# Where GpSimd stops between gathers in a two-layer graph kernel

## The chip, the cores and the metric

The kernel runs on one core of a Trainium2 chip. The metric is the device time of one execution in microseconds (us); lower is better. The kernel before took 847.21 us, the median of three runs (846.74 to 851.41).

## The reference

There are 8 batches of 2048 nodes with 128 features (`x`), and one 2048 x 2048 matrix `adj` that is sparse: the diagonal, and about 8 further entries in a row, placed symmetrically, each with a value of its own.

```python
# layer 0
sj, si = x @ w_j, x @ w_i
res = si[:, :, None] + sj[:, None, :] + adj[None] * w_r + g_b
x = layernorm(x + einsum('bij,bjd->bid', res, x) @ weight + bias)
# layer 1: A = adj, hops of a Chebyshev recursion, A1 = A2 = adj
xs = [x, x A, 2 (x A) A - x, x A, 2 (x A) A - x]
x = layernorm(x + relu(concat(xs) @ Theta1 + bias))
```

In layer 0 the matrix multiplies `x @ weight` (the terms from `si` and `sj` are of low rank and are added as a few rows). Layer 1 becomes two passes over the matrix, here called hops 1 and 2.

## The kernel before, in words

Nodes are cut into 16 chunks of 128; a chunk of all batches is a tile of 128 x 1024 numbers (512 KB). Everything is in 32-bit floats.

The first 150 us load `adj` and `x`, transpose the matrix, find which blocks hold entries, and form Y = `x @ weight` (tiles `Y0` to `Y15`), while chunk 0 of layer 0 is summed along the way. Then a loop `for c in range(ND)` does chunks 1, 2 and 3 of layer 0 with dense products: in step c, TensorE multiplies 16 pairs of tiles for chunk c + 1 (L839, inner loop over j). Beside these products VectorE builds the lists of rows that the other chunks need (`list_round`, L556).

The remaining 12 chunks of layer 0, and all 16 in each hop, use only the rows that matter. For a chunk, seven lists of 128 row numbers are gathered from DRAM: four for strips of 32 nodes, two for strips of 64, one for the whole chunk (`fetch_lists`, L714, which calls `gather`, L640). One gather is one indirect DMA issued by GpSimd; it brings 128 rows of 4 KB into one of nine tiles, `Y0` to `Y8`, used in turn. In layer 0 the rows come from `y0_d` (the profile prints it as `y_d`), in hop 1 from `u_d`, in hop 2 from `y_d`. TensorE multiplies them by the matching rows of the matrix (`listed_rows`, L880).

These matrix rows are gathered too, into four `stage` tiles: `gathers(count, mm)` (L687) takes the next `count` jobs off a list, seven jobs to a chunk, four for the narrow lists and three for the wide ones. In layer 0 they come from `rr_d`; for the four dense chunks, which are needed only from the hops on, from `adj`. With `mm` given, each gather also waits for that matrix product. `keep_r` (L663) multiplies what has landed by a mask on VectorE and moves it to where TensorE reads it. GpSimd runs all gathers in the order in which the program calls them (`behind`, L196, keeps each after the one before).

The order of chunks is `seq`: 9 to 14, then 4 to 8, then 15. In the loop over `seq` each step does: the chunk's own block (L864), `put` (its matrix rows), the wide-list jobs of the next chunk, the listed rows, `make_u` of the chunk before (transposes L184, products L399 and the store of U by ScalarE's queue), then `finish0` (L378: two `tensor_add`, L382, and the layernorm, L204 to L229). Chunk 15 comes last; after it 14 of the 28 jobs of the dense chunks are issued, and the rest in hop 1, two in a step.

A hop opens three chunks (`begin`: L932 and the own block), does the listed rows of the first two, and so on. Within an engine the compiler's scheduler orders instructions by the dependences it is given, except where `keep_in_program_order` or `behind` fix it; so a new dependence can move work on other engines. VectorE and ScalarE read TensorE's results from PSUM, and wait for TensorE's signals to do so.

Of the kernel before, what the change touches and what calls it, by code (L numbers as in the profile page):

```python
# [18 lines left out]
def kernel(  # L19
# [29 lines left out]
    nc = tc.nc  # L49
# [4 lines left out]
    HB = B // 2  # L54
# [7 lines left out]
    ND = 4  # L62
    NG4 = 9

    seq = list(range(NG4, NC - 1)) + list(range(ND, NG4)) + [NC - 1]
    LAST = NC - 1
# [102 lines left out]
    nc.vector.memset(si, 1.0)  # L169

    flip = [0]

    def evict(dst, src, dve=None):
        flip[0] ^= 1
        if flip[0] if dve is None else dve:
            nc.vector.tensor_copy(dst, src)  # L176
        else:
            nc.scalar.copy(dst, src)  # L178

    def transpose4(srcs, name, t=None, dve=None):  # L180

        pt = p_tr.tile([P, 4, P], F32, name=f"pt_{name}", tag="pt")
        for i, s in enumerate(srcs):
            nc.tensor.transpose(pt[:, i, :], s, ident)  # L184
        if t is None:
            t = trp.tile([P, 4, P], F32, name=f"tr_{name}", tag="tr")
        evict(t, pt, dve)
        return t

    def batches_t(src, name, dve=None):  # L190
# [187 lines left out]
    def finish0(c, accs, xr, norm=True):  # L378

        for h in range(2):  # L380
            hs = slice(h * HB, (h + 1) * HB)
            nc.vector.tensor_add(xr[:, hs, :], accs[h], xr[:, hs, :])  # L382
        if norm:
            layernorm(xr, f"0_{c}")
        return xr

    def make_u(c, z, xt, u=None):

        for h in range(2):
            transpose4([z[:, h * HB + i, :] for i in range(4)], f"p{c}_{h}",  # L390
                       xt[:, h * HB:(h + 1) * HB, :])
        if c < ND:
            nc.scalar.dma_start(out=xt_d[c], in_=flat(xt))
        if u is None:
            u = rows4(f"u{c}")
        for h in range(2):
            pp = p_sm.tile([P, HB, D], F32, name=f"pp{c}_{h}", tag="sm")
            for i in range(HB):
                nc.tensor.matmul(  # L399
                    pp[:, i, :], xt[:, h * HB + i, :], th[:, 0, :], start=True, stop=True  # L400
                )
            nc.scalar.copy(u[:, h * HB:(h + 1) * HB, :], pp)
        nc.scalar.dma_start(out=u_d[c * P:(c + 1) * P, :], in_=flat(u))

    def copy_r(n0, n1):
# [275 lines left out]
        (c, q, n) for cs in (seq, range(ND)) for q in (True, False) for c in cs  # L681
        for n in range(4 if q else 3)
    ]
    dense_jobs = 7 * ND
    waiting = []

    def gathers(count, mm=None):  # L687

        for _ in range(count):
            if not jobs:  # L690
                break
            c, q, n = jobs.pop(0)
            if n == 0:
                if len(waiting) == 3:
                    keep_r(*waiting.pop(0))
                waiting.append((
                    c, q, int(c >= ND) + 1,
                    stages[:, turn[1] % 4 * BD:turn[1] % 4 * BD + BD + 4 * TW],
                ))
                turn[1] += 1  # L700
            gather_r(*waiting[-1], n)
            if mm is not None:
                tc.add_manual_dep(
                    order[-1].ins, mm.ins.name,
                    mybir.DependencyInfo(
                        mybir.DependencyClass.Sync, mybir.DependencyReason.DATA
                    ), reason="pace",
                )


    G = [flat(y) for y in Y[:NG4]]
    got = {}

    def fetch_lists(i, src, c, count):  # L714

        gs = got.setdefault((i, c), [])
        ids = [4 * c + t for t in range(4)] + [LP + 2 * c, LP + 2 * c + 1, LF + c]
        if i and c in first:
            src = src[0:LAST * P]
        for n in ids[len(gs):count]:  # L720
            gs.append(G[turn[2] % NG4])
            turn[2] += 1
            gather(gs[-1], src, idx, n, src.shape[0])
        return gs

    def put(c):
# [52 lines left out]
    with nc.allow_non_contiguous_dma(reason="512-byte rows of blocks"):  # L779
        pending, accs, xr = None, acc0, load_x(0, "xr", nc.sync)  # L780
        at1, ar2 = first_at[1], None
        for c in range(ND):
            if c + 1 < ND:
                if NA <= c + 2 < ND:
                    ar2 = load_rows(c + 2, wide[3])
                xr1 = load_x(c + 1, "xr", nc.sync)
            if c < 2:
                copy_r(2 + 5 * c, 7 + 5 * c)
            if 1 <= c <= 2:
                for n in range(8 * c - 8, 8 * c):  # L790
                    tc.keep_in_program_order(
                        nc.sync.dma_start(out=y0_d[n * P:(n + 1) * P, :], in_=flat(Y[n]))
                    )
            if c == 0:
                make_ub()
                more_rows()
                rank1(0, accs, si_t(0))
            else:
                z = finish0(c, accs, xr, c > 2)
            if c + 1 < ND:  # L800
                accs1, sit = acc_pair(), si_t(c + 1)
                at2 = first_at.get(c + 2)
                for j in range(NC):
                    if c == 0:
                        if j == 4:
                            tile_ranks()
                        if j == 7:
                            tile_lists()
                        if j == 10:
                            at = tile_lists_end()  # L810
                            half_ranks()
                        if j == 14:
                            chunk_ranks()
                            z = finish0(c, accs, xr, False)
                            layernorm(z, "0_0", at)
                    if c == 1 and j < 2:
                        candidates(2 * j)
                        candidates(2 * j + 1)
                    if c == 1 and (j > 1 and j % 2 == 0 or j == NC - 1):
                        list_round(j // 2 - (j < NC - 1))  # L820
                    if c == 2:
                        if j == 6:
                            at = chunk_lists_end()
                            layernorm(z1, "0_1", at)
                        if j == 9:
                            layernorm(z, "0_2", at)
                        if j == 8:
                            fetch_own(0, y0_d, seq[0])
                            late0 = fetch_block(0, seq[0])
                    if (c > 0 or j > 11) and not (c == 2 and j > 11):  # L830
                        gathers(1 if j % 4 == 3 else 2, mm)
                    if c == 2 and j > 11:
                        fetch_lists(0, y0_d, seq[0], 2 * j - 22)
                    if ar2 is not None and j % 2 == 0 and j >= 8:
                        if j == 8:
                            at2 = by_chunk(wide[0])
                        transpose_group(c + 2, ar2, at2, j // 2 - 4)
                    for h in range(2):
                        mm = nc.tensor.matmul(  # L839
                            accs1[h], at1[:, j, :], Y[j][:, h * HB:(h + 1) * HB, :],  # L840
                            start=(j == 0), stop=False, skip_group_check=True,
                        )
                rank1(c + 1, accs1, sit)
                if c == 1:
                    gathers(2, mm)
                if c == 2:
                    fetch_lists(0, y0_d, seq[1], NG4 - 7)
                at1, ar2, accs = at2, None, accs1
            if pending is not None:
                make_u(*pending)  # L850
            z1 = z
            pending, xr = (c, z, rows4(f"xt{c}")), xr1
# [37 lines left out]
    with nc.allow_non_contiguous_dma(reason="512-byte rows of a diagonal block"):  # L890
        xr = load_x(seq[0], "xs", nc.sync)
        for c, c1 in zip(seq, seq[1:] + [None]):
# [4 lines left out]
            if c1 is not None:  # L897
                fetch_own(0, y0_d, c1)
                if c1 in first:
                    late0 = fetch_block(0, c1)  # L900
                xr1 = load_x(c1, "xs", nc.sync)
                put(c)
                while any(job[0] == c1 for job in jobs):
                    gathers(1)
            else:
                put(c)
            if c == LAST:
                listed_rows(0, y0_d, c, accs, lambda: make_u(*pending))
            else:
                listed_rows(0, y0_d, c, accs)  # L910
                make_u(*pending)
            z = finish0(c, accs, xr)
            if c == LAST:
                gathers(dense_jobs // 2)
            pending, xr = (c, z, x1t[c], held.get((1, c))), xr1
        for c in hops[:2]:
            fetch_own(1, u_d, c)
# [4 lines left out]
        def hop(i, src):  # L922
# [16 lines left out]
            def end(c, accs):  # L939
# [17 lines left out]
                else:  # L957
# [2 lines left out]
                        out=out[:, c * P:(c + 1) * P, :].rearrange("b p f -> p b f"), in_=z  # L960
                    )

            early = [begin(n) for n in range(3)]
            late = [fetch_block(i, c) for c in first]
            for n in range(2):
# [105 lines left out]
```

## Time and profile before

| | |
|---|---|
| median of three runs | 847.21 us |
| the profiled execution's own time | 891.02 us |
| its span, first to last instruction | 889.2 us |
| mean clock granted to TensorE | 0.965 of full speed |
| TensorE, matrix products | 785.2 us busy, 3631 |
| GpSimd (POOL) | 420.2 us busy, 431 |
| VectorE (DVE) | 360.1 us busy, 1056 |
| ScalarE (ACT) | 176.6 us busy, 429 |
| one gather on GpSimd | 0.99 us, the next starts 1.30 us after it |
| DMA over the span | 264 MB, 297 GB/s |

All durations of engines come from the one profiled execution, which took longer than the runs. In it the dense chunks end at about 273 us, layer 0 at about 493 us, and hop 2 begins at about 709 us. A line of a timeline gives start, busy time, engine, source line, operation, what it writes and reads, how often, and in brackets how long the engine was idle before it and what released it. "remote" or "another core or an unknown queue" stands where no instruction or transfer known to the profile ended at the right moment. A busy interval of GpSimd for a gather is the time in which it issues the gather, not that of the data.

### The profile page before, as it was taken

Reading aid. Unit: us, or ns where it says so; the run is one execution under the profiler, and the core shown is the slowest. Engines: PE = TensorE matmul, PEld = TensorE weight load, DVE = VectorE, ACT = ScalarE, POOL = GpSimd, SP = SyncE. Lnnn points to the kernel's source line nnn. Section 1 sums busy time; section 2 is a strip of 40 time slices with the busy share of each in tenths; the row PEclk is TensorE's granted clock in tenths of the full one; section 3 lists DMA queues with packets and bytes.
Section 4 is the critical chain, followed back from the end, with each engine's and each line's share of the span. In section 5 each row is a group of like instructions: output and inputs, shape, how many; then the busy total and the mean of one; then the engine's idle time right before and its main releaser. Section 6 shows DMA issues by size and latency. Waiting matters only on the chain.

```text
span 889.2 us, 10783 instructions
## 1 busy us (share of the span) xinstructions
PE 785.2 (88%) x3631; PEld 390.2 (44%) x3631; DVE 360.1 (41%) x1056; ACT 176.6 (20%) x429; POOL 420.2 (47%) x431
## 2 busy tenths in 40 slices
PE   5999999999993888799894889998999999999994
PEld 4666654465541533333332533333433434445441
DVE  5555674246960443444441201000100035556666
ACT  3665652001110222221221100000000001111112
POOL 0000000036777267566655475666665456666661
PEclk9999999899997898999997999999999999999998
DMA  8699999892485699899894789999999789999995
GB/s 284 197 312 312 298 299 295 259 364 92 133 305 179 240 340 318 309 334 371 294 355 163 248 266 373 315 329 312 370 382 386 273 308 357 362 342 344 343 351 173
DMA packets 172283, 264.28 MB, mean 297 GB/s; under 512 B 17458, under 2 KB 123226, under 8 KB 170044
## 3 DMA queue, kind: packets, MB, share of 16 engines
q0 software_dynamic: 49280, 147.41, 46.3%
q1 hardware_dynamic: 99610, 88.37, 31.2%
q10 hardware_dynamic: 23330, 27.73, 8.6%
q8 instruction: 31, 0.51, 0.2%
q14 instruction: 32, 0.26, 0.1%
HBM read 242.03 MB, written 60.96 MB: 341 GB/s over the span
## 4 chain that ended last, share of the span: by engine, by line
PE 65%; DMA 11%; issue 8%; DVE 6%; another core or an unknown queue 5%; ACT 3%; POOL 1%; SPq 0%; POOLq 0%; DVEq 0%; ACTq 0%
PE acc L880 26%; PE acc L864 8%; DMA Y<-u_d,idx 6%; PE acc L932 5%; PE acc L839 5%; PE pp L399 4%; PE acc L340 4%; PE acc L330 3%; DMA Y<-y_d,idx 3%; DVE rc L556 2%; PE pt_p L184 2%; PE pt_a L184 2%; DMA rc<-in_adj_dram 1%; PE pt_r L950 1%
## 5 line engine op out<-in xcount | busy, mean ns | idle before, releaser
L641 POOL DMA_INDIRECT Y<-y_d,idx x196 | 194.1, 991 | 141.7 <-PE acc L880 88.1
L880 PE MATMUL acc<-Y,rc 128*32 128x512 f32 (+2 forms) x896 | 227.8, 607 | 17.6 <-DMA Y<-u_d,idx 7.1
L641 POOL DMA_INDIRECT stage<-rr_d,idx x84 | 85.7, 1020 | 222.3 <-PE acc L839 194.2
L641 POOL DMA_INDIRECT Y<-u_d,idx x112 | 111.0, 991 | 76.5 <-PE acc L880 44.4
L880 PEld LDWEIGHTS acc<-Y,rc 128*32 128x32 f32 (+2 forms) x896 | 60.6, 128 | 174.5 <-issue 114.1
L880 PE MATMUL acc<-Y,rct 128*32 128x512 f32 (+2 forms) x336 | 97.6, 619 | 4.0 <-DVE rct L669 3.9
L839 PE MATMUL acc<-Y,wide 128*128 128x512 f32 x192 | 87.9, 608 | 0.0
L864 PE MATMUL acc<-Y,rd 128*128 128x512 f32 x140 | 67.0, 597 | 0.0
L839 PEld LDWEIGHTS acc<-Y,wide 128*128 128x128 f32 x192 | 36.2, 195 | 40.0 <-issue 40.0
L217 ACT ACTIVATE st<-st,epst 128x8 f32<-128x8 f32 x32 | 9.9, 310 | 220.8 <-DVE st L216 100.1
L176 DVE COPY z<-acc 128x512 f32<-128x512 f32 x9 | 6.2, 692 | 117.1 <-remote 33.1
L382 DVE TENSOR_TENSOR xs<-acc,xs 128x512 f32<-128x512 f32 x24 | 16.4, 682 | 75.1 <-PE pp L399 40.4
L880 PEld LDWEIGHTS acc<-Y,rct 128*32 128x32 f32 (+2 forms) x336 | 23.2, 131 | 46.3 <-issue 36.4
L184 PE MATMUL pt_a<-ident,rc 128*128 128x128 f32 x240 | 35.9, 286 | 6.5 <-DMA rc<-in_adj_dram 6.0
L330 PE MATMUL acc<-wx,tr_x 128*128 128x130 f32 x256 | 36.6, 286 | 3.9 <-ACT tr_x L178 3.1
L952 DVE SCALAR_TENSOR_TENSOR z<-z,pt_r 128x512 f32<-128x512 f32 x32 | 20.5, 682 | 47.6 <-PE acc L880 24.4
L301 DVE TENSOR_REDUCE rc<-rc 128x64 f32<-128x2048 f32 x16 | 36.5, 2280 | 7.0 <-DMA rc<-in_adj_dram 7.0
L330 PEld LDWEIGHTS acc<-wx,tr_x 128*128 128x128 f32 x256 | 32.9, 195 | 14.0 <-ACT tr_x L178 6.4
L340 PE MATMUL acc<-Y,wide 128*128 128x512 f32 x64 | 36.1, 646 | 2.5 <-ACT Y L334 1.4
L184 PEld LDWEIGHTS pt_a<-ident,rc 128*128 128x128 f32 x240 | 29.5, 148 | 15.8 <-issue 14.5
L932 PEld LDWEIGHTS acc<-th,wide 128*128 128x128 f32 x256 | 31.7, 194 | 9.8 <-issue 8.8
L309 DVE TENSOR_REDUCE stage<-rct 128x64 f32<-128x2048 f32 x12 | 27.4, 2285 | 20.3 <-ACT rct L178 20.3
(210 smaller groups left out, 918.4 us busy)
## 6 DMA issues: line engine op xcount, KB each, us to landing
rc<-in_adj_dram SPq DMA_DIRECT2D x16, 1024.0 KB
rr_d<-rct SPq DMA_DIRECT2D x12, 1024.0 KB
rr_d<-in_adj_dram SPq DMA_DIRECT2D x12, 1024.0 KB
xs<-in_x_dram SPq DMA_DIRECT2D x20, 512.0 KB
y_d<-Y SPq DMA_DIRECT2D x16, 512.0 KB
out_dram<-z ACTq DMA_DIRECT2D x16, 512.0 KB
u_d<-u ACTq DMA_DIRECT2D x14, 512.0 KB
Y<-y_d SPq DMA_DIRECT2D x14, 512.0 KB
```

The costliest lines, as they stand in the source:

```text
L184: nc.tensor.transpose(pt[:, i, :], s, ident)
L301: nc.vector.tensor_reduce(mk[:, c, :], a.rearrange("p (w f) -> p w f", f=TW), AX.X, ALU.max, apply_absolute_value=True,)
L309: nc.vector.tensor_reduce(mkt[:, :, 4 * c:4 * c + 4], at.rearrange("p j (t f) -> p j t f", f=TW), AX.X, ALU.max, apply_absolute_value=True,)
L330: nc.tensor.matmul(py[:, i, 0:D + 2], xt[b // HB][:, (b + i) % HB, :], wx, start=True, stop=True,)
L340: nc.tensor.matmul(acc0[h], first_at[0][:, c, :], Y[c][:, h * HB:(h + 1) * HB, :], start=(c == 0), stop=False, skip_group_check=True,)
L399: nc.tensor.matmul(pp[:, i, :], xt[:, h * HB + i, :], th[:, 0, :], start=True, stop=True)
L641: g = nc.gpsimd.indirect_dma_start(out=out, out_offset=None, in_=src, in_offset=bass.IndirectOffsetOnAxis(ap=ids[:, n:n + 1], axis=0), bou ...
L839: mm = nc.tensor.matmul(accs1[h], at1[:, j, :], Y[j][:, h * HB:(h + 1) * HB, :], start=(j == 0), stop=False, skip_group_check=True,)
L864: in_order(nc.tensor.matmul(accs[h], r, t[:, h * HB:(h + 1) * HB, :], start=start, stop=stop, skip_group_check=True,))
L880: in_order(nc.tensor.matmul(accs[h][w * t:w * t + w], r[:, o + w * t:o + w * t + w], gs[t][:, h * HB * D:(h + 1) * HB * D], start=False, s ...
L932: in_order(nc.tensor.matmul(accs[h][:, b, :], x1t[c][:, h * HB + b, :], th[:, i, :], start=(b == 0), stop=False, skip_group_check=True,))
L952: nc.vector.scalar_tensor_tensor(z[:, hs, :], z[:, hs, :], 0.0, pt, op0=ALU.max, op1=ALU.add)
```

## The change

It does five things.

1. `evict`, `finish0` and `make_u` now keep the instruction that they issue in a table `done`: the last eviction of a `transpose4`, the second `tensor_add` of a chunk, the last copy of U.
2. A helper `pace` makes the gather that was just issued wait for a given instruction. `gathers` uses it as before for `mm`; `fetch_lists` can use it for its first gather.
3. In the dense loop's step c = 2, matrix-row gathers stop after j = 8, and the first Y0 gathers begin at j = 10 instead of j = 12. Four matrix-row gathers less stand before them: 54 instead of 58.
4. In the loop over `seq`, the first of the next chunk's wide-list gathers waits for the `tensor_add` of the chunk two before the current one (for seq[1] that is chunk 3; seq[0] has none).
5. At the end of layer 0 there were 14 gathers of dense chunks' rows in one go, then nine gathers of U. Now five gathers are issued before chunk 15 is finished, one that waits for its `tensor_add`, and one more; then, as hop 1 opens, four lists of U for the first chunk, three that wait for the last transposed tile's eviction, two lists of the second chunk that wait for the last copy of U, and then seven more gathers of dense chunks' rows.

The data, the arithmetic and the number of gathers are the same. On VectorE, the six `keep_r` instructions that stood before chunk 3's two `tensor_add` now stand after that chunk's layernorm.

```diff
+    done = {}
     def evict(dst, src, dve=None):
         flip[0] ^= 1
         if flip[0] if dve is None else dve:
-            nc.vector.tensor_copy(dst, src)
-        else:
-            nc.scalar.copy(dst, src)
+            return nc.vector.tensor_copy(dst, src)
+        return nc.scalar.copy(dst, src)
...
-        evict(t, pt, dve)
+        done["t"] = evict(t, pt, dve)
...
-            nc.vector.tensor_add(xr[:, hs, :], accs[h], xr[:, hs, :])
+            done[c] = nc.vector.tensor_add(xr[:, hs, :], accs[h], xr[:, hs, :])
...
-            nc.scalar.copy(u[:, h * HB:(h + 1) * HB, :], pp)
+            done["u"] = nc.scalar.copy(u[:, h * HB:(h + 1) * HB, :], pp)
...
-    dense_jobs = 7 * ND
     waiting = []
+
+    def pace(ins):
+
+        tc.add_manual_dep(
+            order[-1].ins, ins.ins.name,
+            mybir.DependencyInfo(mybir.DependencyClass.Sync, mybir.DependencyReason.DATA),
+            reason="pace",
+        )
...
             gather_r(*waiting[-1], n)
             if mm is not None:
-                tc.add_manual_dep(
-                    order[-1].ins, mm.ins.name,
-                    mybir.DependencyInfo(
-                        mybir.DependencyClass.Sync, mybir.DependencyReason.DATA
-                    ), reason="pace",
-                )
+                pace(mm)
...
-    def fetch_lists(i, src, c, count):
+    def fetch_lists(i, src, c, count, step=None):
...
             gather(gs[-1], src, idx, n, src.shape[0])
+            if step is not None:
+                pace(step)
+                step = None
         return gs
...
-                    if (c > 0 or j > 11) and not (c == 2 and j > 11):
+                    if c == 2 and j > 5:
+                        if j < 9:
+                            gathers(2, mm)
+                        elif j > 9:
+                            fetch_lists(0, y0_d, seq[0], 2 * j - 18)
+                    elif c > 0 or j > 11:
                         gathers(1 if j % 4 == 3 else 2, mm)
-                    if c == 2 and j > 11:
-                        fetch_lists(0, y0_d, seq[0], 2 * j - 22)
...
                 put(c)
+                step = done[([ND - 1] + seq)[seq.index(c) - 1]] if c != seq[0] else None
                 while any(job[0] == c1 for job in jobs):
-                    gathers(1)
+                    gathers(1, step)
+                    step = None
...
+            if c == LAST:
+                gathers(5)
             z = finish0(c, accs, xr)
             if c == LAST:
-                gathers(dense_jobs // 2)
+                gathers(1, done[c])
+                gathers(1)
...
+            if i == 1:
+                fetch_lists(i, src, first[0], 4)
+                fetch_lists(i, src, first[0], 7, done["t"])
+                fetch_lists(i, src, first[1], NG4 - 7, done["u"])
+                gathers(7)
             early = [begin(n) for n in range(3)]
```

## The prediction

> **What bounds the kernel now.** I read the page, then the chain of work that ended last, then the timelines of single engines around the chain's two longest pieces. The page first:
>
> ```profile
> PE 785.2 (88%) x3631; PEld 390.2 (44%) x3631; DVE 360.1 (41%) x1056; ACT 176.6 (20%) x429; POOL 420.2 (47%) x431
> ...
> PE 65%; DMA 11%; issue 8%; DVE 6%; another core or an unknown queue 5%; ACT 3%; POOL 1%; SPq 0%; POOLq 0%; DVEq 0%; ACTq 0%
> ```
>
> TensorE carries two thirds of the chain; what the change can reach is in the rest. An "unknown queue" holding 4.7% on a one-core kernel (about 42 us) is odd. The chain in order of time (start, length, what) says where it is:
>
> ```profile
> 269.39 21.39 another core or an unknown queue
> ...
> 470.74 13.03 another core or an unknown queue
> ...
> 513.75 5.30 DMA Y<-u_d,idx
> ```
>
> Two gaps hold 34 us: one where layer 0 leaves its dense chunks (c = 3), one at the last sparse chunk but one. The third line is a price: a 512 KB gather, from its start on GpSimd to its landing. Now the timelines at the first gap (start, busy, engine, line, what, idle before and its releaser):
>
> ```profile
> 272.74 1.09 PE L184 MATMUL pt_p<-ident,xr 128*128 128x128 f32 x8
> ...
> 286.79 0.99 POOL L641 DMA_INDIRECT Y<-y_d,idx  x1 [0.30 <-issue]
> ...
> 290.76 0.69 DVE L382 TENSOR_TENSOR xr<-acc,xr 128x512 f32<-128x512 f32 x1 [21.37 <-remote]
> ...
> 291.08 0.59 ACT L178 COPY xt<-pt_p 128x512 f32<-128x512 f32 x1 [24.59 <-remote]
> ...
> 293.02 3.79 PE L399 MATMUL pp<-th,xt 128*128 128x128 f32 x16 [18.33 <-DVE xt L176]
> ```
>
> TensorE finished the transposes that ScalarE wants at 273.8, and before them the sums that VectorE wants; both readers start 17 us later, within 0.32 us of each other, and TensorE then waits 18.3 us for them. In between GpSimd gathers without a break, its last one ending at 287.78. The second gap has the same shape:
>
> ```profile
> 471.84 0.44 PE L184 MATMUL pt_p<-ident,xs 128*128 128x128 f32 x2
> ...
> 480.82 0.99 POOL L641 DMA_INDIRECT stage<-in_adj_dram,idr  x1 [0.30 <-issue]
> ...
> 483.79 0.69 DVE L176 COPY Y<-pt_p 128x512 f32<-128x512 f32 x1 [13.05 <-remote]
> ...
> 484.54 3.79 PE L399 MATMUL pp<-th,Y 128*128 128x128 f32 x16 [11.26 <-DVE Y L176]
> ```
>
> Readers of TensorE's results resume 3.0 and 2.0 us after GpSimd's last gather. Smaller cases agree: gathers end at 315.80, 330.59, 808.94, 851.29 and a reader on ScalarE or VectorE starts at 317.38, 332.26, 810.34, 852.66 (1.4 to 1.7 us later), though its input had been done for 4 to 8 us. Early in a run of gathers results arrive at once (384.37, two gathers in). So in this execution a long unbroken run of gathers goes with late arrival of TensorE's signals, and a break lets them through. I take that as the trace's rule, not as a known mechanism.
>
> **What the Trainium skill says.** "SBUF — State Buffer", section "SBUF: two separate sides": only VectorE's shared port pair is contended with GpSimd; ScalarE and TensorE have ports of their own. ScalarE waited here as long as VectorE, so the trace doesn't fit a port lock. "Perfetto Trace Analysis", section "Summary: the profiler window per engine type": a TensorE end is an estimate, and a software-issued DMA ends in the record when its descriptors are written, not when data lands. Hence 990 ns for a 512 KB gather, and I take landings from the chain. "DMA: Bandwidth & Descriptors", section "Anatomy of one DMA": 2.0 us plus bytes at 436 GB/s, which would be an estimated 3.2 us for 512 KB; the trace has 5.30, with other transfers beside it, and I use that.
>
> **Part 1, first Y0 gathers sooner.** Of the row gathers of `rr_d`, 58 stood before the first Y0 gather, now 54: the first nine Y0 gathers move up four places. GpSimd starts one every 1.30 us (0.99 busy, 0.30 issue) without waiting there, so Y0 starts at 271.21 instead of 276.42 and the ninth ends at 282.6 instead of 287.8: 5.2 us. The stores they depend on don't hold them: they waited for nothing at 276.42, and the traffic of those stores had faded by 262. Next stands the first gather of chunk 11, which now waits for the second `tensor_add` of chunk 3, so GpSimd stops at 282.6. By the rule VectorE and ScalarE resume 2 to 3 us later, near 285.1 instead of 290.76: 5.7 us sooner. VectorE's `keep_r` work moves behind chunk 3's layernorm; its six products are 1.2 us and TensorE needs them only in the 64-row products about 10 us on: nothing. At the resumed end three `stage` gathers stand before the five Y0 gathers of chunk 10 (none before), but those wait for TensorE reading their buffers, 11 us later: hidden. One gather more (three for chunk 12, two before) then delays chunk 11 by 1.3 us. Left: 4.4 to 5.7, I take **4.8 us**.
>
> **Part 2, one pause per chunk.** The first row gather of chunk seq[k+1] waits for the add of seq[k-2]. Behind it on GpSimd stand two row gathers and the lists of the chunk. In the even stretch from 372 to 457 the row gather starts at 387.95 and the add ends at 389.80: 1.85 us of pause each. GpSimd idles 2.51 us per chunk there, waiting for TensorE to free buffers; that shrinks to about 0.7. The period is 15.19 us, TensorE's products and a 1.35 us wait for the layernorm, so the pause costs nothing; without that idle time it would cost up to 1.85 x 8 = 15 us. Before 345 the add is already done when GpSimd arrives: no pause and no gain.
>
> **Part 3, end of layer 0.** Of 14 `stage` gathers after the last lists (463.92 to 481.81) five stay; the sixth waits for chunk 15's add. GpSimd stops at 470.1, so the copy at 483.79 starts at about 472.3, when its input is done: 11.5 us. The end of chunk 15's products goes from 492.2 to 480.7 and its add from 492.9 to 481.5. Then two gathers (to 484.1), four of U (to 489.3), three behind `done["t"]`, two behind `done["u"]`. Those steps shift from 501.8 and 506.7 to 487-491 and 491-495. The last two end near 498, and seven `stage` gathers (7 x 1.30 = 9.1 us) follow, to 507. Only then come the five U gathers of chunk 10, which started at 512.46. TensorE could have freed their buffers by 501; the seven in front of them eat 6 of the 11.5. Left: **5.5 us**.
>
> Sum: 4.8 + 0 + 5.5 = 10.3 us of the profiled execution's 891.0 (span 889.2 and 1.8 around it), so 880.7. That execution is 43.8 us, 5.2%, over the median of the runs, 847.2. Is the stall in the plain runs too? The trace can't say. It is the value that decides. Bounds: all of it there (10.3 gained) or none (below). I take all of it, since nothing in the trace ties the stall to recording: 847.2 - 10.3 = **836.9**.
>
> **Rivals.** *The stalls belong to the profiled execution (0.35, ends slower).* For it: the unknown queue's 42 us nearly equals the 43.8 us between profile and median. Against it: TensorE emits as many records in the even stretch, where the readers are seldom late. Without stalls, GpSimd's order alone counts. Part 1 gives 1.3 us (17 gathers instead of 18 up to chunk 10's lists), at most 4.5. In part 3 chunk 15's products end at about 479, U's first nine gathers are all out by 493.5 before the change and 496 after it; before, the next five start when buffers come free at 496.5, after it behind the seven `stage` gathers at 505: 8.5 us lost, in a stretch (530 to 575) where TensorE is 90% busy and gives nothing back. Net 4 to 7: about 852 us, 846 to 855. If a share f of the stalls is real, the sum is 10.3f - 5.5(1 - f): slower begins below f = 0.35.
>
> *A wait takes the place of the one removed (0.15).* GpSimd resumes right behind the add, and the next run of gathers makes signals late again (from 304 to 345 runs of nine or ten do so, and no pause falls there). Or U's seven `stage` gathers cost the whole of part 3. One of the two gains is left: 842, 839 to 848.
>
> *The pauses don't pause.* In the even stretch the wait is 1.85 us at most and elsewhere satisfied; then only the moved gathers act. This is inside the cases above, since both large stops (282.6 and 470.1) wait for adds that can't be done yet.
>
> **How the numbers follow.** Forecast 0.50: 837, own range 829 to 843. Stall only in the profile 0.35: 852. Wait replaced 0.15: 842. 0.5% is 4.2 us, about what three runs of this kernel (846.7 to 851.4) can tell from no change: faster is below 843.0, slower above 851.4. Faster: 0.47 + 0.08 + 0.02 = 0.57. Same: 0.03 + 0.07 + 0.13 = 0.23. Slower: 0.20 from the profile-only case. The range has to reach into that case, so 829 to 853 leaves out about 0.05 below and 0.1 above.
>
> **What would show it.** In the profile after: GpSimd idle at about 282 to 287 and 470 to 481; VectorE's add of chunk 3 near 285 and chunk 8's copy near 472; the unknown queue down from 4.7% to about 2%; a period still 15.2 us per chunk; the five U gathers of chunk 10 behind seven `stage` gathers near 507. If the readers still resume only when some later gather ends, the rule is wrong. If the span falls by 10 us or more and the median doesn't, the stall was the profiled execution's own. If the period grows, part 2 isn't hidden.

## The result and the profile after

The changed kernel took 860.07 us, the median of four runs (859.11 to 861.89), against 847.37 us for the kernel before: ratio 1.013, 95% interval 1.0098 to 1.0162. It is 1.3% slower, where a faster kernel at 836.9 us was forecast, with a range of 829 to 853. Here and below a ratio compares only the runs within 1.5% of the fastest of the same kernel, while a median takes all runs. Its profiled execution took 859.31 us (span 857.4, clock 0.984), in line with its runs; that of before had taken 891.02. So the profiled span fell by 32 us while the median rose by 12.7. The prediction had named this as the sign that the stall belonged to the profiled execution alone.

The page of after, its busy row and its chain of waits:

```profile
PE 778.1 (91%) x3631; PEld 382.4 (45%) x3631; DVE 360.4 (42%) x1056; ACT 176.6 (21%) x429; POOL 419.5 (49%) x431
...
PE 53%; DMA 28%; issue 9%; DVE 3%; POOL 3%; ACT 3%; POOLq 0%; SPq 0%; DVEq 0%; ACTq 0%
```

The unknown queue, 5% before, is gone, and DMA has gone from 11% to 28% of the chain. The timelines at the first gap (start, busy, engine, line, what, idle before and its releaser):

```profile
267.96 0.99 POOL L641 DMA_INDIRECT Y<-y_d,idx  x1 [0.30 <-issue]
...
269.86 0.69 DVE L382 TENSOR_TENSOR xr<-acc,xr 128x512 f32<-128x512 f32 x1 [6.99 <-PE acc L373]
...
271.74 0.58 ACT L178 COPY xt<-pt_p 128x512 f32<-128x512 f32 x1 [8.98 <-PE pt_p L184]
...
290.84 0.99 POOL L641 DMA_INDIRECT Y<-y_d,idx  x1 [0.30 <-DMA stage<-rr_d,idx]
297.96 1.00 POOL L641 DMA_INDIRECT stage<-rr_d,idx  x1 [6.13 <-DVE xs L382]
```

VectorE adds chunk 3 and ScalarE copies the transposes within about 0.1 us of TensorE's results (the last term of the sums, L373, runs from 268.77 to 270.68 in two halves, the transposes end at 271.72), in the middle of a run of gathers that GpSimd issues without a pause. The rule of the prediction, that such a run makes signals late, does not hold in this execution. GpSimd's first long stop begins at 291.8 and lasts 6.13 us; it waits for the add of chunk 9. The chain of waits there, in order of time, names what was late instead:

```profile
272.36 7.02 DMA xt_d<-xt
...
279.95 17.43 DMA rd<-rr_d
297.43 2.07 PE acc L872 x2
```

And at the end of layer 0:

```profile
448.53 1.00 POOL L641 DMA_INDIRECT stage<-in_adj_dram,idr  x1 [0.30 <-DVE xs L227]
459.49 1.00 POOL L641 DMA_INDIRECT stage<-in_adj_dram,idr  x1 [9.96 <-DVE xs L382]
...
483.99 1.00 POOL L641 DMA_INDIRECT Y<-u_d,idx  x1 [0.96 <-DMA stage<-in_adj_dram,idr]
...
488.02 1.90 PE L888 MATMUL acc<-Y,rc 128*32 128x512 f32 x2 [3.69 <-DMA Y<-u_d,idx]
```

GpSimd idles 10 us for chunk 15's add; the five U gathers of chunk 10 come at 483.99, behind seven adjacency gathers (473.75 to 483.02), and TensorE waits 3.69 us for them.

### The profile page after: what moved, and what is told of

Same layout as the page of the kernel before. It is cut to its first block, busy times and chain, and to the rows that moved or that the text cites. A ratio compares the mean times of both kernels' runs of the same rounds, so it can differ in the third digit from the quotient of the medians.

```text
span 857.4 us, 10772 instructions
## 1 busy us (share of the span) xinstructions
PE 778.1 (91%) x3631; PEld 382.4 (45%) x3631; DVE 360.4 (42%) x1056; ACT 176.6 (21%) x429; POOL 419.5 (49%) x431
## 4 chain that ended last, share of the span: by engine, by line
PE 53%; DMA 28%; issue 9%; DVE 3%; POOL 3%; ACT 3%; POOLq 0%; SPq 0%; DVEq 0%; ACTq 0%
PE acc L888 18%; DMA Y<-u_d,idx 11%; DMA Y<-y_d,idx 11%; PE acc L847 7%; PE acc L872 5%; PE acc L340 4%; PE acc L330 4%; PE pp L399 3%; POOL Y L641 3%; PE acc L945 3%; DMA rd<-rr_d 2%; PE pt_a L184 2%; DVE rc L556 2%; PE pt_p L184 2%; DMA rc<-in_adj_dram 1%
## 5 line engine op out<-in xcount | busy, mean ns | idle before, releaser
L847 PE MATMUL acc<-Y,wide 128*128 128x512 f32 x192 | 87.7, 607 | 0.0
L964 DVE TENSOR_TENSOR z<-acc,b1bc 128x512 f32<-128x512 f32 x32 | 21.5, 687 | 43.4 <-PE acc L872 28.6
L641 POOL DMA_INDIRECT stage<-in_adj_dram,idr x28 | 28.0, 999 | 18.7 <-DVE xs L382 10.0
```

The source lines that it names most:

```text
L641: g = nc.gpsimd.indirect_dma_start(out=out, out_offset=None, in_=src, in_offset=bass.IndirectOffsetOnAxis(ap=ids[:, n:n + 1], axis=0), bou ...
L847: mm = nc.tensor.matmul(accs1[h], at1[:, j, :], Y[j][:, h * HB:(h + 1) * HB, :], start=(j == 0), stop=False, skip_group_check=True,)
L964: nc.vector.tensor_add(z[:, hs, :], accs[h], b1bc.to_broadcast([P, HB, D]))
```

## Experiments

What was expected before each run is printed below, word for word. The letters A to G in it name rival explanations; each is spelled out where it first stands.

### The same kernel on several chips

The kernel before was run unchanged three times with a profile of its own, and after twice more. The groups of runs came from four chips, numbers 1, 5, 12 and 14; only chip 14 served twice.

> The kernel before, unchanged, profiled a second time. Theory A (the two long stalls of VectorE and ScalarE belonged to that one profiled execution): time 847 us, ratio 1.00, but this profile has a span near 845 us instead of 889.2, no piece of an unknown queue over 3 us in the chain, and chunk 3's add and chunk 8's copy start within 1 us of their inputs although GpSimd gathers without a break. Theory B (long runs of gathers make TensorE's signals late whenever a profile is taken): the stalls of about 21 and 13 us come back at the same two places and the span is again 885 to 892.

> The changed kernel, unchanged, beside the kernel before on one chip. Theory E (there are two conditions of a chip: one in which long runs of gathers make signals late and before takes about 894 us, one without and before takes 847): if before takes about 894 us here, after gains what the forecast summed, 5 to 12 us, ratio 0.987 to 0.995, with chunk 8's copy near 475 instead of 483; if before takes about 847 us here, ratio 1.010 to 1.016 again. Theory F (after is slower by its order of gathers, wherever it runs): ratio 1.010 to 1.016 here in either case.

> The kernel before, unchanged, once more, for its profile on a chip where it takes about 848 us. Theory G (signals are prompt on that chip): span near 846, no unknown queue in the chain, chunk 3's add near 271, U's five lists of chunk 10 issued right as buffers come free, first copy of hop 1 near 490 (after: 502). Where before takes about 894 us: the stalls of 17 to 21 and 11 to 13 us for the third time.

> The changed kernel once more. Where before takes about 894 us: parts 2 and 3 gained 4.7 and 7.6 us each alone there and part 1 nothing, so 880 to 886, ratio 0.985 to 0.993; the pauses of part 2 let part 1 gain too, which speaks for the lower end. Where before takes about 848 us: 860, ratio 1.013.

> The kernel before, unchanged, for its profile on a chip where it takes about 848 us. Theory G (signals are prompt there): span near 846, no unknown queue in the chain, chunk 3's add near 271, chunk 9's near 293, first copy of hop 1 near 490 (after: 499 to 502). Where before takes about 894 us: the stalls once more.

| chip | before, median us | before, lowest to highest us | after, median us | after / before (95%) |
|---|---|---|---|---|
| 1 | 893.99 (67 runs) | 883.52 to 900.54 | not run | |
| 5 | 894.70 (45) | 887.37 to 901.73 | 884.95 | 0.9892 (0.9813 to 0.9970) |
| 14 | 848.94 and 848.81 (32, 32) | 844.98 to 852.76 | 860.22 | 1.0135 (1.0081 to 1.0189) |
| 12 | 848.79 (24) | 844.78 to 853.54 | not run | |

The two groups of chips don't overlap. On chip 1 both stalls of the profile of before come back. On chip 5 the second does (10.36 us of unknown queue in the chain), but the first, forecast at 17 to 21 us, is short: GpSimd's run broke off for 2.95 us there, and chunk 3's add starts at 275.64, about 4 us after its sums were done. On chip 14 there are no stalls. Since the plain runs on chips 1 and 5 take as long as the profiled ones, the stalls are not made by the profiler. Before on chip 1, the chain and then the timelines:

```profile
271.77 17.66 another core or an unknown queue
...
470.93 11.00 another core or an unknown queue
```

```profile
285.39 0.99 POOL L641 DMA_INDIRECT Y<-y_d,idx  x1 [0.30 <-issue]
...
289.41 0.69 DVE L382 TENSOR_TENSOR xr<-acc,xr 128x512 f32<-128x512 f32 x1 [17.64 <-remote]
```

Before on chip 14:

```profile
PE 58%; DMA 26%; issue 7%; DVE 3%; ACT 3%; POOL 2%; SPq 0%; POOLq 0%; ACTq 0%; DVEq 0%
```

So most of what the first two pages differ in, the unknown queue and the share of DMA, is the chip and not the change.

```profile
269.58 0.69 DVE L382 TENSOR_TENSOR xr<-acc,xr 128x512 f32<-128x512 f32 x1 [3.46 <-PE acc L373]
...
272.91 1.00 POOL L641 DMA_INDIRECT Y<-y_d,idx  x1 [0.30 <-issue]
...
289.95 0.99 POOL L641 DMA_INDIRECT Y<-y_d,idx  x1 [5.69 <-PE acc L880]
...
296.84 1.02 PE L864 MATMUL acc<-Y,rd 128*128 128x512 f32 x2
```

Theory E holds and theory F falls: the sign of the change depends on the chip. That a chip keeps its kind is shown for chip 14 alone. Theory A's "one execution" and theory B's "whenever a profile is taken" are both wrong, as the lateness goes with the chip. The 891.02 us of the profile of before fits chips 1 and 5, and its median of 847.21 us fits chips 12 and 14, as after's first 860.07 fits chip 14. I infer that profile and median of before came from chips of different kinds; the numbers of those chips are not known.

The granted clock explains little of this difference. Its mean is lower on chips 1 and 5 (0.968 in both profiles, 0.984 on chip 14), but not everywhere: from 372 to 457 us it is 1.00 on all three, from 240 to 300, around the first stall, 0.86, 0.97 and 0.91, and from 457 to 500, around the second, 0.84, 0.84 and 1.00. TensorE is busy for 779.3 us on chip 1, 790.9 on chip 5 and 779.1 on chip 14, so products that run slower make up at most 12 of the 45 us between the times.

The adds of the chunks show where the 45 to 48 us between the two kinds of chip go. From chunk 2's add to chunk 14's, before takes 141.3 to 144.5 us in its three profiles with stalls and 118.7 on chip 14; from chunk 8's to chunk 15's it takes 27.1 to 27.2 and 14.1; the rest is lost in the hops. The length of the first stall hardly matters for the first of these sums: 142.8, 144.5 and 141.3 us go with 45.4, 45.5 and 31.5 us from chunk 2's add to chunk 3's. Chunk 9's add then follows chunk 3's after 15.7 us on chip 1, where the stall was long, and after 26.0 on chip 5, where it was short (25.7 on chip 14). So of the 14 us by which the first stalls differ, about 4 are left at chunk 9's add.

On chip 5, after does what the forecast worked out:

```profile
286.09 0.99 POOL L641 DMA_INDIRECT Y<-y_d,idx  x1 [0.30 <-issue]
...
290.19 0.69 DVE L382 TENSOR_TENSOR xr<-acc,xr 128x512 f32<-128x512 f32 x1 [13.66 <-remote]
...
470.50 1.00 POOL L641 DMA_INDIRECT stage<-in_adj_dram,idr  x1 [0.30 <-DVE xs L227]
...
473.33 0.69 DVE L177 COPY Y<-pt_p 128x512 f32<-128x512 f32 x1 [1.20 <-PE acc L888]
...
507.04 1.00 POOL L641 DMA_INDIRECT Y<-u_d,idx  x1 [0.30 <-issue]
```

GpSimd stops at 287.1 and at 471.5; the readers follow 3.1 and 1.8 us later. The unknown queue is 3% of the chain, and the last five U gathers begin at 507.04, where the forecast had put them ("near 507").

### One part at a time

Part 1 alone is the new condition in the dense loop:

```diff
+                    if c == 2 and j > 5:
+                        if j < 9:
+                            gathers(2, mm)
+                        elif j > 9:
+                            fetch_lists(0, y0_d, seq[0], 2 * j - 18)
```

> Before with part 1 alone: the first Y0 gathers four places sooner. Theory C (the loss is a collision: 512 KB gathers started sooner fill the DMA queues ahead of chunk 9's x rows and its block of rr_d, for which TensorE waited 7.36 us in the profile of after): 853 to 855 us, that is 6 to 8 us lost, with the wait on the block of rr_d in the profile. Theory D (the loss sits at the end of layer 0, behind the seven adjacency gathers): 846 to 847 us.

> Part 1 alone, once more. Where before takes about 848 us: Theory C (part 1's early Y0 gathers cost what parts 1 and 2 together lost, 3.9 us): 851 to 853, chunk 9's add near 297 against 293 in before. Rival (part 2's pauses cost it, GpSimd waiting 5 to 6 us for chunk 9's add behind chunk 10's lists): 848 to 849. Where before takes about 894 us: as in the first run, 893.

> Part 1 alone, a third time. Where before takes about 849 us: if part 1 only makes part 2's pause bind (with both, GpSimd waits 5.3 us for chunk 9's add ahead of chunk 12's row gathers, in a stretch where it has no idle time to give), part 1 alone is 848 to 850; if the earlier Y0 gathers cost by themselves, 851 to 854. Where before takes about 894 us: 893 to 895 as twice measured.

Part 2 alone is the pause per chunk:

```diff
+                step = done[([ND - 1] + seq)[seq.index(c) - 1]] if c != seq[0] else None
-                    gathers(1)
+                    gathers(1, step)
+                    step = None
```

> Before with part 2 alone: one pause of GpSimd for each sparse chunk, order of gathers as before. As forecast (the pause is hidden in GpSimd's idle 2.5 us per chunk): 847 us, ratio 0.999 to 1.001. Rival (in an execution without stalls GpSimd is behind somewhere and the pause is paid): 1 to 1.85 us in each of up to 8 chunks, 850 to 860 us.

> Part 2 alone. Where before takes about 848 us: the even stretch keeps its 15.2 us a chunk in after, so nothing is lost there; up to 3.9 us (parts 1 and 2 together) if GpSimd's wait for chunk 9's add holds up the row gathers and lists behind it: 848 to 852. Where before takes about 894 us: 887 to 892, as measured once.

Part 3 alone is the end of layer 0 and the opening of hop 1:

```diff
+                gathers(5)
             z = finish0(c, accs, xr)
-                gathers(dense_jobs // 2)
+                gathers(1, done[c])
+                gathers(1)
...
+                fetch_lists(i, src, first[0], 4)
+                fetch_lists(i, src, first[0], 7, done["t"])
+                fetch_lists(i, src, first[1], NG4 - 7, done["u"])
+                gathers(7)
```

> Before with part 3 alone: the other order of gathers and the pauses at the end of layer 0. Theory D (U's five lists of chunk 10 start behind seven adjacency gathers): 853 to 856 us, 6 to 8.5 lost. Theory C (the loss is part 1's collision): 849 us at most, since GpSimd reaches those five gathers at 484 in the profile of after and TensorE waits for them only 3.7 and 1.4 us there.

> Part 3 alone, once more. Where before takes about 848 us: after less parts 1 and 2 leaves 7 us for part 3, so 854 to 856, with TensorE waiting 4 to 6 us for U's lists of chunk 10 behind seven adjacency gathers (my forecast for a chip without stalls was 8.5 lost). Rival (part 3 costs only beside the other two): 848 to 850. Where before takes about 894 us: 886, as in the first run.

> Part 3 alone. Where before takes about 848 us: after less parts 1 and 2 leaves 7 us for part 3, so 854 to 856, with TensorE waiting 4 to 6 us for U's lists of chunk 10 behind seven adjacency gathers (my forecast for a chip without stalls was 8.5 lost). Rival (part 3 costs only beside the other two): 848 to 850. Where before takes about 894 us: 885 to 887, as twice measured.

| alone | chips 1 and 5 | chip 14 or 12 |
|---|---|---|
| part 1 | 1.0015 (0.9991 to 1.0039), 1.0018 (0.9993 to 1.0044) | 1.0041 (0.9996 to 1.0086) |
| part 2 | 0.9936 (0.9900 to 0.9973) | 1.0001 (0.9979 to 1.0023) |
| part 3 | 0.9923 (0.9892 to 0.9954), 0.9898 (0.9867 to 0.9929) | 1.0080 (1.0051 to 1.0109) |

Part 3 carries both signs. On chip 1 it removes the second stall entirely. Timelines of part 3 there:

```profile
471.67 1.00 POOL L641 DMA_INDIRECT stage<-in_adj_dram,idr  x1 [0.30 <-DVE xs L227]
...
474.55 0.69 DVE L177 COPY Y<-pt_p 128x512 f32<-128x512 f32 x1 [1.27 <-PE acc L885]
...
512.21 1.92 PE L885 MATMUL acc<-Y,rc 128*32 128x512 f32 x2 [5.34 <-DMA Y<-u_d,idx]
```

From the add of chunk 8 to that of chunk 15, the next in order, it takes 14.1 us, as on chip 14, instead of 27.1 in the profiles of before on chips 1 and 5. Of these 13.0 us, TensorE's wait for the lists of chunk 10 takes back about 4: from chunk 15's add to VectorE's first copy of hop 1 it takes 42.6 us instead of 38.4 to 39.1. On chip 14 there is no stall to remove and only that loss is left. Part 3 on chip 14, and before on chip 14 under it:

```profile
479.69 0.99 POOL L641 DMA_INDIRECT Y<-u_d,idx  x1 [0.82 <-DMA stage<-in_adj_dram,idr]
...
483.90 1.91 PE L885 MATMUL acc<-Y,rc 128*32 128x512 f32 x2 [3.86 <-DMA Y<-u_d,idx]
```

```profile
471.43 0.99 POOL L641 DMA_INDIRECT Y<-u_d,idx  x1 [1.55 <-PE acc L880]
...
482.09 6.37 PE L880 MATMUL acc<-Y,rc 128*32 128x512 f32 x22 [0.21 <-DMA Y<-u_d,idx]
```

The two executions reach chunk 15's add within 0.1 us of each other (454.8). The five U gathers then start 8.3 us later. TensorE's wait costs 4.5 us (VectorE's first copy of hop 1 at 494.7 instead of 490.2), and hop 1 adds 2.3 by its last copy (580.4 instead of 573.6). The rest of the difference of these two profiles comes later and is not in the medians: 0.80% of 848.8 is 6.8 us. So theory D holds for part 3, and theory C's forecast of 849 us at most for it was wrong.

Part 1 alone gave nothing on chips 1 and 5: its Y0 gathers do start sooner, but without part 2's pause three matrix-row gathers follow at once, the run ends at 288.2, and the reader resumes at 291.67. On chip 12 its interval just includes no change; the next runs place its loss.

Part 2's gain on chip 1 (0.64%, and 4.7 us between the medians) was not expected. Its one profile is ahead of the three of before by chunk 9's add already (52.5 us after chunk 2's, where they take 57.5 to 61.7), and up to there no added wait has held GpSimd: what broke GpSimd's run just ahead of the Y0 gathers, for 2.95 us, is a wait at a matrix-row gather, and before has the same break in its profile on chip 5. Whether part 2 brings this about stays open.

### Parts 1 and 2, and the order without the waits

The first is after with the end of layer 0 as before; the second is after with `step` left out everywhere, so that the order of gathers stays and no gather waits for a step.

> Parts 1 and 2 together, the end of layer 0 as before. Where before takes about 894 us: part 1 alone gave nothing there because three more gathers ran on behind the Y0 gathers and readers resumed 3 us behind the last; with part 2's pause in place the run ends three gathers sooner than with part 1 alone, readers resume 2 to 3 us after the first of those stops, near 286, and the time is 3 to 6 us under part 1 alone. Rival (the run goes on, as chunk 11's pause is not reached): as part 1 alone, 893. Where before takes about 847 us: Theory C (collision of the early Y0 gathers with chunk 9's loads) gives 853 to 856, Theory D 847 to 848.

> After with its order of gathers kept and every added wait on a step taken out. Where before takes about 894 us: if the pauses carry the gain, it is lost and the time is 889 to 897; if the order alone carries it (at the end of layer 0 the first U gather has to wait for a buffer anyway, so GpSimd stops seven gathers earlier without a pause), region two gains 6 to 8 us as in the run of part 3 and the time is within 3 us of after's. Where before takes about 847 us: the same as after within 2 us, as no pause binds for longer than GpSimd is idle, or less than after if the pauses are what costs.

Both ran on chip 14: parts 1 and 2 together 853.10 us, 1.0046 (1.0031 to 1.0061), that is 3.9 us lost; the order without waits 854.89 us, 1.0071 (1.0046 to 1.0096), 6.0 us lost, against 11.5 (0.0135 of 848.9) for after beside it. So about half the loss is in the order. The intervals of order and after overlap a little (1.0081 to 1.0096), and the other half, the waits, is less certain.

Theory C named the collision rightly. With part 1 the Y0 gathers start 5.1 us sooner (21.8 us after chunk 2's add in part 1 on chip 12, 26.9 in before on chip 14), so that they are in the DMA queues when ScalarE stores chunk 2's transposed x. That store took 7.02 us in after and 6.54 in part 1 alone. SyncE's load of chunk 9's x rows waits for that store: in before on chip 14 it started 3.2 us after the store was issued (275.30 behind 272.07), in after 7.2 us (279.52 behind 272.36). Behind it in SyncE's queue stands the block of `rr_d` for chunk 10, which in after lands 17.43 us after its start. TensorE waits 7.36 us for it in after, 6.45 with parts 1 and 2, 4.65 with part 1 alone, and not at all in before. Before on chip 14, and after under it:

```profile
275.30 0.39 SPq L235 DMA_DIRECT2D xs<-in_x_dram  x1
```

```profile
279.52 0.39 SPq L235 DMA_DIRECT2D xs<-in_x_dram  x1
...
297.43 2.07 PE L872 MATMUL acc<-Y,rd 128*128 128x512 f32 x2 [7.36 <-DMA rd<-rr_d]
```

But the collision only takes back what the sooner gathers had gained. Chunk 9's listed products, which they serve, end at 289.2 instead of 296.1; chunk 10 then starts at 297.43 instead of 296.84. The loss shows two chunks later. Among the profiles without stalls, chunk 12's add comes 91.9 to 97.8 us after chunk 2's in the five with part 1's order, and 87.7 to 90.7 us after it in the four with before's. In between GpSimd idles more: from 262 us to chunk 13's last list, the time beyond the usual 0.30 us between gathers sums to 9.8 to 12.8 us in the five and to 6.3 to 10.5 in the four. In before on chip 14 the DMA engines are busy for 98 to 100% of the time from 275 to 345 us; with part 1 alone it is 89% from 300 to 324. So the idle time of GpSimd is likely what is lost, but this is argued. A rival is not tested: part 1 also gave TensorE another order at chunk 12, five of chunk 11's eight transposes ahead of the 64-row products instead of one, and no run has the one without the other.

With parts 1 and 2 together some of GpSimd's idle time is the pause, again on chip 14:

```profile
298.53 1.00 POOL L641 DMA_INDIRECT stage<-rr_d,idx  x1 [5.32 <-DVE xs L382]
...
308.45 0.99 POOL L641 DMA_INDIRECT Y<-y_d,idx  x1 [3.60 <-PE acc L888]
```

With part 1's order GpSimd comes to chunk 12's first row gather at 293.2, and chunk 9's second add begins at 297.6. With part 2 alone it came there at 298.9, when that add was ending, and waited 2.63 us for chunk 10's add one gather group later (315.15), which its median does not show. But part 1 without the pause waits 8.51 us for the buffer in the second line instead, so the pause adds little: 3.9 us together, 3.5 for part 1 alone.

### One added wait

```diff
             if c == LAST:
-                gathers(dense_jobs // 2)
+                gathers(5)
+                gathers(1, done["t"])
+                gathers(8)
```

This is before with one wait more; no engine has another order.

> Before with a single added wait and no other order on any engine: of the fourteen adjacency gathers at the end of layer 0 the sixth waits for the last copy of chunk 8's transposes. Where before takes about 894 us: if the break lets TensorE's signals through, the copy that came 10 to 13 us late starts within 3 us of the fifth gather, and the time is 885 to 888, part 3's whole gain without its order; if not, 894 or more. Where before takes about 849 us: part 3's loss was the seven gathers ahead of U's lists, so this one is 848 to 851; if the pause was the loss, 854.

It ran on chip 12: 849.99 us against 848.79, 1.0012 (0.9994 to 1.0031).

```profile
444.84 0.99 POOL L641 DMA_INDIRECT stage<-in_adj_dram,idr  x1 [3.04 <-ACT Y L178]
...
471.28 0.98 POOL L641 DMA_INDIRECT Y<-u_d,idx  x1 [2.67 <-PE acc L885]
```

A pause of 3 us here is hidden: the U gathers of chunk 10 still wait for their buffers. So a pause of this length is not part 3's loss. By the timelines that loss is the seven gathers ahead of U's lists, together with the 10 us for which GpSimd idles for chunk 15's add instead of issuing them; no run has part 3's order without its pauses and without part 1. Whether this one wait takes part 3's gain on chips 1 and 5 was not measured.

### Two attempts at a better kernel

The first holds the nine Y0 gathers for chunk 3's add, keeps parts 2 and 3, and spreads the seven adjacency gathers over hop 1 (`gathers(3)` in a step instead of 2, none at its opening). The second is before with the same wait ahead of the Y0 gathers, and the break of the last section.

```diff
             if c == ND - 1:
+                fetch_lists(0, y0_d, seq[0], 7, done[c])
+                fetch_lists(0, y0_d, seq[1], NG4 - 7)
```

> Part 1 taken back, all nine first Y0 gathers held until chunk 3's add instead; part 2 and part 3 kept, but the seven adjacency gathers ahead of chunk 10's U lists spread over hop 1, three a chunk instead of two. Where before takes about 894 us and runs of gathers do make signals late: chunk 3's add starts about 2 us after the last row gather (near 277 instead of 289) and hop 1 opens 5 us sooner than with part 3 alone: 868 to 876 us, well under before and after. If the stall doesn't hang on GpSimd's run, the add stays at about 289 and the Y0 gathers come later still: 890 to 900. Where before takes about 847 us: 844 to 848.

> Before's order of gathers with two breaks only: the first Y0 gather waits for chunk 3's add, and after five of the fourteen adjacency gathers at the end of layer 0 the sixth waits for the last copy of chunk 8's transposes. Where before takes about 894 us: if a break lets signals through, chunk 3's add starts within 3 us of the last row gather, near 277 to 279, and chunk 8's copy near 474 instead of 483: 10 and 8 us less, 872 to 880. If the signals are late for another reason, both breaks only push gathers back: 894 to 905. Where before takes about 848 us: both waits are satisfied or fall into idle time of GpSimd: 846 to 851.

Both ran on chip 14 and both lost: 860.99 us, 1.0140 (1.0089 to 1.0191), and 857.21 us, 1.0102 (1.0063 to 1.0141). The wait for chunk 3's add was satisfied when GpSimd came to it, yet from chunk 2's add to chunk 12's they took 94.0 and 94.4 us, before 88.8: with the gathers moved, the scheduler gave TensorE another order there, so these two runs don't measure the pause alone. Spreading the seven gathers restored hop 1's opening (35.3 us from chunk 15's add to VectorE's first copy; before 35.4, part 3 39.9), but from that copy to the end of hop 2's first adds it took 195.8 us instead of 188.8. The places in which before issues the seven, while GpSimd would wait for U's buffers anyway, cost nothing; as a third gather in each step of hop 1 they seem to cost these 7 us. No version that beats before on both kinds of chip was found.

## Why the prediction was wrong

**The step that failed** is "I take all of it, since nothing in the trace ties the stall to recording: 847.2 - 10.3". The stall was real, and in plain runs too, but only on chips where before takes 894 us. The median that I subtracted from came, by its time, from a chip without it. There the runs showed the change's costs alone: 6.8 us lost by part 3 and 3.9 by parts 1 and 2. The evidence was on the table: the unknown queue's 42 us nearly equal the 43.8 us between profile and median. I put that down as "for" the rival and still gave the stall 0.65. A gain that exists only inside a gap between profile and median can't be taken off the median.

**The likeliest case, against the chips that stall.** After gains 9.7 us on chip 5 (894.70 to 884.95), where the sum said 10.3, but the terms are others, so that the near match is luck. Part 1's 4.8 are not there alone (1.0015 and 1.0018). With part 2's pause the stop comes as described, and in after on chip 5 the reader follows it 3.1 us later. But I let 5.7 us less of stall pass to the end almost whole, and the three profiles of before with stalls speak against that: chunk 3's add 14 us sooner moved chunk 14's by 1.5 to 3.2 us. Part 2's 0 was 4.7 to 5.7 us gained on chip 1; why is open. Part 3's 5.5 were 6.9 and 9.1: it removes 13.0 us of stall (I had 11.5), and the seven gathers take back about 4 (I had 6).

**The rival that came true** ("the stalls belong to the profiled execution") had the right sign, and for a chip without stalls the right mechanism in part 3, but 852 instead of 860. That the stalls are the profiled execution's own is not right: they are the chip's. Its terms against the runs on chips 12 and 14: part 3, 8.5 lost forecast, 6.8 measured; part 2, nothing forecast, nothing measured (1.0001); part 1, 1.3 to 4.5 gained forecast, 3.5 lost measured alone and 3.9 with part 2. The last is the mis-sized one, by 5 us or more. I counted GpSimd's places and missed that the same nine gathers of 512 KB stand in the DMA queues ahead of a store, and so ahead of two loads of SyncE, one of which TensorE needs; this undoes the gain. What turns it into a loss two chunks on is not fully shown. 3.9 + 6.8 = 10.7 us, against 11.5 beside it on chip 14 and 12.7 in the first measurement.

**"Before 345 the add is already done when GpSimd arrives"** was read from a trace in which GpSimd was the one held up. On chip 14 it waits 2.63 us for chunk 10's add with part 2 alone, at no measured cost, and in after, in both profiles without stalls, 6.13 and 6.02 us for chunk 9's.

**What held.** The period of the even stretch is 15.2 us a chunk in after, as forecast (359.58 to 374.78 in the chain). The U gathers at 507.04, the copy at 473.33 (472.3 forecast) and chunk 15's second add at 480.5 (481.5) hold on the stalling chip. That GpSimd's run and the late reader go together holds there in the main: at the two long stalls of before and after on chips 1 and 5 VectorE resumed 1.4 to 3.1 us behind the last gather. It is no strict rule, though. With part 3 on chip 5 chunk 3's add started at 285.68, in a run of gathers that went on from 278.34 to 291.02; chunk 8's copy on chip 1 started 2.4 us before the end of the run with part 1 and 1.6 with part 2. *A wait takes the place of the one removed* came true for one of the two gains on chip 5: at the end of layer 0 no new stall comes, but the chain of after has 6.14 us of unknown queue at 343, and the 9.7 us gained there are about what part 3 gains there alone (9.1).

## What to carry to other kernels

When the profiled execution is 5% longer than the runs, price a change twice, once with the stalls and once without, and let the likeliest case be the one that the median can contain. A stall that is shortened passes to the end only as far as the work behind it was waiting for it: here 14 us at the stall became 1.5 to 3.2 us twelve chunks on. A gather moved forward is also moved ahead of every store and load that is issued while it is in the queues: follow those to the engine that needs them, not only the engine that issues the gather. And a slot taken from an idle engine has to be given back at a place where that engine is idle too.

## What was not expected of the hardware

- Chips differ by 5% on the same program: 894 us on two, 849 us on two others. The difference is not in the work: GpSimd's gathers take 0.99 to 1.00 us, the even stretch 15.2 us a chunk on both, and TensorE's products 779.3 us in all on chip 1 and 779.1 on chip 14.
- On the slower kind TensorE's own work can be held up during a run of gathers, but is not always: in before on chips 1 and 5 these eight transposes run in 1.09 us. Part 1 on chip 1, and then on chip 12:

```profile
274.98 0.77 PE L184 MATMUL pt_p<-ident,xr 128*128 128x128 f32 x5
276.63 0.27 PE L184 MATMUL pt_p<-ident,xr 128*128 128x128 f32 x1 [0.89 <-issue]
278.76 0.27 PE L184 MATMUL pt_p<-ident,xr 128*128 128x128 f32 x1 [1.86 <-issue]
280.91 0.37 PE L184 MATMUL pt_p<-ident,xr 128*128 128x128 f32 x1 [1.89 <-issue]
```

```profile
273.16 1.09 PE L184 MATMUL pt_p<-ident,xr 128*128 128x128 f32 x8
```

  The last three, and the two products behind them, start 2.1 us apart. What delays them, and why only on some chips, no run here shows.
